# Layer 2's involution pass: queues in the order of the text, norm chains in two steps a turn

## The chip, the cores and the metric

The kernel runs on one core of one Trainium2 chip. The metric is the device time of one execution in microseconds (us). The kernel before took 11256.58 us, the median of three runs (11229.98 to 11261.98). A profile is one further execution under the hardware profiler; its instruction times are shown in us from the start of its span.

Five engines have queues of their own and run each queue in order: TensorE (PE, with its weight loads PEld), VectorE (DVE), ScalarE (ACT), GpSimd (POOL) and SyncE (SP), which in this kernel issues all the DMAs.

## The reference

Sixteen images of 64 x 64 pixels and 256 channels, in float32, go through four layers, each of the form `x = x + layer(group_norm(x))`. Only layer 2 matters here, with the end of layer 1 in front of it and the start of layer 3 behind it:

```python
# end of layer 1: batch norm, relu, residual
x = x + relu((x2 - mean) * rsqrt(var + eps) * gamma + beta)
# layer 2, an involution 3 x 3 with 16 groups, on g = group_norm(x)
r   = relu(bn(g @ Wr + br))                    # 256 -> 64
w   = (r @ Ws + bs).reshape(B, H, W, 16, 1, 9) # 9 weights for each pixel and group
xi  = g @ Wi + bi                              # 256 -> 256
out = sum(w * patches3x3(xi), axis=-1)         # 9 products for each output value
x   = x + out
# layer 3 begins with group_norm(x)
```

`group_norm` has 32 groups of 8 channels over all pixels of an image, so nothing that uses a normalised image can start before the last pixel of that image is known.

## The kernel before

Layer 2 is one loop, a software pipeline. An image is cut into 8 chunks of 512 pixels, and a turn of the loop does four jobs on four different chunks (`jobs`, with the lags 0, 9, 17 and 27 turns of `LAG`):

- `end_of_layer1`, in three parts divided by `yield`: VectorE scales x1 by the spatial factors pf (L899, two instructions); ScalarE applies the relu (L905) and GpSimd adds the residual (L908) to give x2, which is stored; VectorE takes statistics of x2 (L914). With an image's last chunk the chain `norm2` is started.
- `projected`: TensorE multiplies x2 by the scaled Wi (L948, tile px), and ScalarE writes the result with its bias into the padded image `pad` (L952).
- The involution, whose inputs are made one turn earlier by `prepare`: `reduced2` (L969, tile pr; ScalarE's relu L972 to rt), `patches` (TensorE transposes shifted rows of `pad`, L995; ScalarE copies them to xs, L999 to L1005) and `weights` (L979, tile pw, one for each half of the channels). In the turn itself `residual` (L1021 and L1023) puts x2 transposed into PSUM tiles lo, `products` (L1033, 12 VectorE instructions for a half, tile pd) multiplies patches and weights, `sums_on_tensor` (L1050, 18 matmuls) sums the nine taps of one quarter of the first half into lo, and `sums` reduces the rest on VectorE (L1045) and adds lo (L1046). A turn later ScalarE copies the quarter that TensorE summed (L1175), `turned` transposes the result back (L1060, ScalarE copies it to c3, L1061) and hands out its stores, and `statistics3` takes statistics (L1080), which with an image's last chunk starts the chain `norm3`.
- `centred`: GpSimd subtracts the mean for layer 3 (L1103), and 32 DMAs of 22 or 28 KB write the result into `strips`, layer 3's overlapping columns.

The stores of a turn are collected in the list `stores` and issued by SyncE at the start of the next turn (L1150), behind the loads for that next turn (`loads`, L867) and ahead of `load_centred` (tile xc). Most loaded tiles have two buffers; a load waits until all that use the older tile of its slot are done.

`norm2` and `norm3` are generators, as is `group_norm` which they call: group means and deviations through small matmuls with gmat (L117 and L126, tiles pg and pv), an inverse square root with GpSimd's power (L99), then the scaled weights (L924, L925) and their biases (L931, tile pm; L936 and L938), or for `norm3` the saved means and scales (L1087, L1088) and a broadcast of the mean (L1092, L1095 with tile pb, L1098). `step()` moves each running chain to its next `yield`; the loop calls it six times a turn.

None of this text order binds. A scheduler in the compiler orders each engine's queue by dependencies and its own estimates of durations, and takes the order of the text only as a preference. In the trace the queues therefore differ from the text: VectorE's reductions (L1045) stand behind the statistics L914, and pr stands behind `sums_on_tensor`.

[...] the pool `tr` has two (transposes pt, and px), `sm` one (pr and all small tiles of the chains), `pwp` three (pw) and `acc` two (lo).

Of the kernel before, what the change touches and what calls it, by code (L numbers as in the profile page):

```python
# [15 lines left out]
P = 128  # L16
# [28 lines left out]
def network(ctx: ExitStack, tc: tile.TileContext, a: dict, out: bass.AP):  # L45
# [60 lines left out]
            if next(c, c) is c:  # L106
                chains.remove(c)

    def group_norm(stats, pool):


        mv = small.tile([P, 2, 2], F32, tag="gn_mv", name="gn_mv")
        for h in range(2):
            nc.vector.bn_aggr(mv[:, h, :], stats[:, h].rearrange("p n s -> p (n s)"))
        yield
        pg = pool.tile([P, CT], F32, tag="sm", name="pg")
        nc.tensor.matmul(pg[:, 0:2], lhsT=gmat, rhs=mv[:, :, 0], start=True, stop=True)  # L117
        gm = small.tile([P, 2], F32, tag="gn_m", name="gn_m")
        nc.vector.tensor_copy(gm, pg[:, 0:2])
        dev = small.tile([P, 2], F32, tag="gn_d", name="gn_d")  # L120
        nc.vector.tensor_tensor(dev, mv[:, :, 0], gm, ALU.subtract)
        nc.vector.tensor_tensor(dev, dev, dev, ALU.mult)
        nc.vector.tensor_tensor(dev, dev, mv[:, :, 1], ALU.add)
        yield
        pv = pool.tile([P, CT], F32, tag="sm", name="pv")
        nc.tensor.matmul(pv[:, 0:2], lhsT=gmat, rhs=dev, start=True, stop=True)  # L126
        rstd = small.tile([P, 2], F32, tag="gn_r", name="gn_r")
        inv_sqrt(rstd, pv[:, 0:2], GN_EPS)
        yield
        return mv, gm, rstd  # L130

    def normalised(dst, src, gm, rstd, nb):
# [16 lines left out]
    with ExitStack() as st:  # L149
# [80 lines left out]
                chains.append(norm0(i))  # L230

        def norm0(i):
            _, gm, rstd = yield from group_norm(st0.pop(i), sm)
            nb = small.tile([P, 2], F32, tag="gn_b", name="gn_b")
            nc.vector.tensor_tensor(nb, gm, rstd, ALU.mult)
            nc.vector.tensor_scalar(nb, nb, -1.0, None, ALU.mult)
            gn0[i] = (gm, rstd, nb)
# [215 lines left out]

        def gate1(i):

            mv, gm, rstd = yield from group_norm(st1.pop(i), sm)
            av = small.tile([P, 2, 2], F32, tag="av", name="av")
            nc.vector.tensor_copy(av[:, :, 0], mv[:, :, 0])
            nc.vector.tensor_reduce(av[:, :, 1], mxs.pop(i), AX.X, ALU.max)
            for h in range(2):  # L460
                nc.vector.tensor_scalar(
                    av[:, h, :], av[:, h, :], gm[:, h : h + 1], rstd[:, h : h + 1],
                    ALU.subtract, ALU.mult,
                )
            yield
            ph = sm.tile([P, CT], F32, tag="sm", name="ph")
            for h in range(2):
                nc.tensor.matmul(
                    ph[0:16, 0:2], lhsT=w1T[:, h, :], rhs=av[:, h, :], start=(h == 0), stop=(h == 1)
                )  # L470
            hr = small.tile([16, 2], F32, tag="hr", name="hr")
            nc.vector.tensor_scalar(hr, ph[0:16, 0:2], 0.0, None, ALU.max)
            hs = small.tile([16, 1], F32, tag="hs", name="hs")
            nc.vector.tensor_tensor(hs, hr[:, 0:1], hr[:, 1:2], ALU.add)
            yield
            pg = sm.tile([P, CT], F32, tag="sm", name="pgate")
            for h in range(2):
                nc.tensor.matmul(
                    pg[:, h : h + 1], lhsT=w2T[:, h * P : (h + 1) * P], rhs=hs, start=True, stop=True
                )  # L480
            gate = small.tile([P, 2], F32, tag="gate", name="gate")
            nc.scalar.activation(gate, pg[:, 0:2], AF.Sigmoid)
            nc.vector.tensor_tensor(ab[:, 0, i, :], rstd, gate, ALU.mult)
            nc.vector.tensor_tensor(gate, gm, ab[:, 0, i, :], ALU.mult)
            nc.vector.tensor_scalar(ab[:, 1, i, :], gate, -1.0, None, ALU.mult)
            nc.vector.tensor_copy(gm1[:, i, :], gm)
# [335 lines left out]
    with ExitStack() as st:  # L822
# [1 line left out]
        wk = st.enter_context(tc.tile_pool(name="b_work", bufs=2))  # L824
        xs_p = st.enter_context(tc.tile_pool(name="b_xs", bufs=6))
        pd_p = st.enter_context(tc.tile_pool(name="b_pd", bufs=2))
        tr = st.enter_context(tc.tile_pool(name="b_tr", bufs=2, space=PSUM))
        sm = st.enter_context(tc.tile_pool(name="b_sm", bufs=1, space=PSUM))
        pwp = st.enter_context(tc.tile_pool(name="b_pw", bufs=3, space=PSUM))
        acc = st.enter_context(tc.tile_pool(name="b_acc", bufs=2, space=PSUM))  # L830
        gmb = {}
# [60 lines left out]
        def end_of_layer1(i, rc):  # L892
# [21 lines left out]
                nc.vector.bn_stats(st0[i][:, h, rc, :], x2[:, h])  # L914
            if rc == NCH - 1:
                chains.append(norm2(i))

        def norm2(i):

            _, gm, rstd = yield from group_norm(st0.pop(i), sm)  # L920
            wrs = wk.tile([P, 2, 64], F32, tag="wrs", name="wrs")
            w = wk.tile([P, 2, C], F32, tag="wis", name="wis")
            for h in range(2):
                nc.vector.tensor_scalar(wrs[:, h], wr2[:, h], rstd[:, h : h + 1], None, ALU.mult)  # L924
                nc.vector.tensor_scalar(w[:, h], wi[:, h], rstd[:, h : h + 1], None, ALU.mult)  # L925
            yield
            pm = sm.tile([P, CT], F32, tag="sm", name="pm")
            for f in range(3):
                for h in range(2):
                    lhsT = wrs[:, h] if f == 2 else w[:, h, f * P : (f + 1) * P]  # L930
                    nc.tensor.matmul(  # L931
                        pm[0 : 64 if f == 2 else P, f : f + 1], lhsT=lhsT, rhs=gm[:, h : h + 1],
                        start=(h == 0), stop=(h == 1),
                    )
            b2 = small.tile([64, 1], F32, tag="b2", name="b2")
            nc.vector.tensor_scalar(b2, pm[0:64, 2:3], sb2[0:64, 2:3], sb2[0:64, 1:2], ALU.mult, ALU.add)  # L936
            bis = small.tile([P, 2], F32, tag="bis", name="bis")
# [24 lines left out]
        def reduced2(i, rc):  # L962
# [1 line left out]
            wrs, b2, _, _ = gn2[i]  # L964
            rt = rts[rc % 2]
            x2 = taken("x2r")
            pr = sm.tile([P, CT], F32, tag="sm", name="pr")
            for h in range(2):
                nc.tensor.matmul(  # L969
                    pr[0:64, :], lhsT=wrs[:, h, :], rhs=x2[:, h], start=(h == 0), stop=(h == 1)  # L970
# [105 lines left out]
        def statistics3(i, rc, c3):  # L1076
# [3 lines left out]
                nc.vector.bn_stats(st3[i][:, oh, rc, :], c3[:, oh].rearrange("p g t -> p (g t)"))  # L1080
            if rc == NCH - 1:
                chains.append(norm3(i))

        def norm3(i):

            _, gm, rstd = yield from group_norm(st3.pop(i), sm)
            nc.vector.tensor_copy(gm3[:, i, :], gm)  # L1087
            nc.vector.tensor_copy(rs3[:, i, :], rstd)  # L1088
            gmb[i] = wk.tile([P, C], F32, tag="gmb", name="gmb", bufs=1)
# [1 line left out]
            for h in range(2):  # L1091
                nc.vector.tensor_scalar(dg[:, h], ident, gm3[:, i, h : h + 1], None, ALU.mult)  # L1092
            yield
            pb = sm.tile([P, CT], F32, tag="sm", name="pb")
            nc.tensor.matmul(  # L1095
                pb[:, 0:C], lhsT=ones, rhs=dg.rearrange("p h c -> p (h c)"), start=True, stop=True
            )
            nc.vector.tensor_copy(gmb[i], pb[:, 0:C])  # L1098

        def centred(i, rc):  # L1100
# [20 lines left out]

        LAG = (0, 9, 17, 27)
        TURNS = NI * NCH + LAG[3]

        def jobs(n):
# [11 lines left out]
            if end:  # L1139
                load_layer1(*end)  # L1140

        loads(0)
        ahead, made, ending, last_end = None, None, None, None
        for n in range(TURNS):
            end, proj, inv, cen = jobs(n)
            nxt = jobs(n + 1)[2]
            done, stores[:] = list(stores), []
            loads(n + 1)
            for dst, src in done:
                nc.sync.dma_start(out=dst, in_=src)  # L1150
            nxt_cen = jobs(n + 1)[3]
            if nxt_cen:
                load_centred(*nxt_cen)
            now, ahead = ahead, None
            last_end, ending = ending, end_of_layer1(*end) if end else None
            if ending:
                next(ending)
            if last_end:
                next(last_end, None)
            if inv:  # L1160
                w1 = weights(now[1], 1)
                x3 = wk.tile([P, 4, C], F32, tag="x3", name="x3", bufs=3)
            step()

            def prepare():
                x2r, rt = reduced2(*nxt)
                ahead = [x2r, rt]
                ahead.append(patches(*nxt, lambda: ahead.append(weights(rt, 0))))
                return ahead

            if nxt and nxt[1]:
                ahead = prepare()
            step()
            if made:
                nc.scalar.copy(made[2][:, 0:ON_PE, 0:P], made[3][:, 0:ON_PE])  # L1175
            if ending:
                next(ending)
            if inv:
                los = residual(now[0])
            c3 = turned(*made[:3]) if made else None  # L1180
            step()
            if proj:
                projected(*proj)
            if inv:
                pd = products(0, now[2], now[3])
                sums_on_tensor(pd, los[0])
            step()
            if nxt and not nxt[1]:
                ahead = prepare()
            if inv:  # L1190
                pd1 = products(1, w1, now[3])
                sums(0, pd, los[0], x3)
            if made:
                statistics3(*made[:2], c3)
            step()
            if inv:
                sums(1, pd1, los[1], x3)
            made = (*inv, x3, los[0]) if inv else None
            step()
            if cen:  # L1200
                centred(*cen)
        for dst, src in stores:
            nc.sync.dma_start(out=dst, in_=src)

    gates.close()

# [306 lines left out]
```

## Time and profile before

| | |
|---|---|
| median of three runs | 11256.58 us |
| the profiled execution | 11230.29 us |
| its span, first to last instruction | 11228.4 us |
| mean granted clock of TensorE | 0.878 |
| busy over the span: PE, PEld, DVE, ACT, POOL | 76%, 55%, 67%, 42%, 9% |
| layer 2, first L899 to last store of strips | 4169 to 8042 us |
| first products L1033, last sum L1046 | 4286.70 us, 7883.35 us |

A row of a view gives the start, the length, the engine, the line of the kernel, the operation, the tile written and the tile read, their shapes, and how many alike are merged; brackets hold the idle time of the engine just before and what ended it. A row of the waits reads: who waited, for whom, how many us in total, how often, and the longest. The rows that follow busy time by stretch are explained where they are shown. SPq marks a DMA issue on SyncE's queue.

### The profile page before, as it was taken

What the parts mean: (1) busy time and instruction counts of PE and PEld (TensorE: products, weight loads), DVE (VectorE), ACT (ScalarE), POOL (GpSimd) and SP (SyncE); (2) the same over time, 40 slices, a digit from 0 to 9 for tenths busy, and PEclk for the clock granted to TensorE, in tenths of its full rate; (3) what the DMA queues carried; (4) which work ended last, traced back from release to release, by engine and by line L of the source; (5) the groups of instructions that cost most, each with busy time, mean ns of one, the idle gap of its engine ahead of it and who ended that gap; (6) DMA issues with size and microseconds to landing.
All of it is one profiled execution on the core that took longest, in us unless ns stands there. A gap on an engine that the chain in (4) does not pass through costs nothing.

```text
span 11228.4 us, 218020 instructions
## 1 busy us (share of the span) xinstructions
PE 8510.5 (76%) x88184; PEld 6175.2 (55%) x88184; DVE 7531.5 (67%) x11694; ACT 4699.1 (42%) x10571; POOL 1065.1 (9%) x681
## 2 busy tenths in 40 slices
PE   8889888988886407777777777777277777778777
PEld 5666666666664205555555555555165656666555
DVE  5566656656665498988888888899254545555444
ACT  4555555555554004333333333333144444444444
POOL 0110111111110001111111111111000000000000
PEclk9999999999997558888888888888689998998988
DMA  7334334434432385555555555544356555555555
GB/s 239 129 134 148 130 122 146 139 128 133 145 101 84 106 279 177 160 169 165 163 159 167 160 168 164 163 151 141 107 177 202 185 194 179 179 181 176 195 185 171
DMA packets 1353714, 1796.58 MB, mean 160 GB/s; under 512 B 132875, under 2 KB 1031812, under 8 KB 1351556
## 3 DMA queue, kind: packets, MB, share of 16 engines
q1 hardware_dynamic: 1352708, 1782.63, 49.6%
q8 instruction: 697, 11.42, 0.4%
q14 instruction: 309, 2.53, 0.1%
HBM read 1268.05 MB, written 536.87 MB: 161 GB/s over the span
## 4 chain that ended last, share of the span: by engine, by line
PE 32%; DVE 20%; issue 17%; DMA 10%; ACT 9%; SPq 7%; POOL 4%; POOLq 0%; DVEq 0%; ACTq 0%
PE pa L1347 6%; DVE wm L1303 6%; SPq L1150 5%; PE pq L261 5%; PE pk L1288 4%; PE py L417 4%; DMA c_d<-c 3%; DVE x L1045 3%; PE pr L1256 2%; ACT sq L426 2%; ACT wm L1298 2%; DVE pd L1033 2%; PE px L948 2%; PE pt L995 2%; DMA xc<-x_d 1%
## 5 line engine op out<-in xcount | busy, mean ns | idle before, releaser
L261 PE MATMUL pq<-wq,xn 128*128 128x384 f32 x4096 | 1475.9, 500 | 59.8 <-DVE diag L310 20.9
L1033 DVE TENSOR_TENSOR pd<-xs,pw 128x576 f32<-128x576 f32 (+15 forms) x3072 | 1450.5, 544 | 47.7 <-ACT xs L1001 47.7
L1303 DVE TENSOR_TENSOR wm<-pk,spanb 128x704 f32<-128x704 f32 x896 | 1148.4, 1344 | 217.4 <-PE pk L1288 217.1
L1288 PE MATMUL pk<-rt,span 64*128 64x176 f32 x12288 | 1175.6, 329 | 153.5 <-DVE wm L1303 61.0
L1347 PE MATMUL pa<-wm,xw 126*32 126x48 f32 x45056 | 819.6, 227 | 474.2 <-issue 374.1
L1288 PEld LDWEIGHTS pk<-rt,span 64*128 64x128 f32 x12288 | 938.1, 188 | 385.7 <-ACT wm L1298 181.8
L1298 ACT ACTIVATE wm<-pk,spanb 128x176 f32<-128x176 f32 x2560 | 975.0, 542 | 337.8 <-PE pk L1288 328.9
L1045 DVE TENSOR_REDUCE x<-pd 128x384 f32<-128x3456 f32 (+1 forms) x256 | 1109.2, 4334 | 0.0
L1347 PEld LDWEIGHTS pa<-wm,xw 126*32 126x32 f32 x45056 | 679.8, 124 | 714.2 <-issue 516.7
L1357 DVE SCALAR_TENSOR_TENSOR ex<-pa,msk,ex 128x192 f32<-128x192 f32 x704 | 287.2, 416 | 1161.8 <-ACT ex L1356 1159.3
L261 PEld LDWEIGHTS pq<-wq,xn 128*128 128x128 f32 x4096 | 752.8, 194 | 492.5 <-issue 54.1
L995 PE MATMUL pt<-ident,pad 128*128 128x128 f32 x4608 | 759.7, 310 | 244.2 <-ACT pad L952 188.5
L995 PEld LDWEIGHTS pt<-ident,pad 128*128 128x128 f32 x4608 | 593.4, 160 | 422.0 <-ACT pad L952 234.2
L1050 PE MATMUL lo<-pd,ident 128*128 128x128 f32 x2304 | 568.0, 415 | 285.4 <-DVE pd L1033 285.4
L999 ACT COPY xs<-pt 128x512 f32<-128x512 f32 x1152 | 644.8, 586 | 299.1 <-PE pt L995 264.4
L1356 ACT ACTIVATE ex<-pa,msk 128x192 f32<-128x192 f32 x704 | 289.3, 420 | 1019.2 <-PE pa L1347 1016.1
L1050 PEld LDWEIGHTS lo<-pd,ident 128*128 128x128 f32 x2304 | 501.2, 268 | 335.6 <-DVE pd L1033 315.3
L948 PE MATMUL px<-x2p,wis 128*128 128x512 f32 x1024 | 571.7, 708 | 37.5 <-ACT c L1061 23.2
L972 ACT ACTIVATE rt<-pr,b,sb 64x512 f32<-64x512 f32 x128 | 98.9, 772 | 1077.3 <-PE pr L969 1017.5
L417 PE MATMUL py<-wo,oT 128*128 128x256 f32 x2048 | 482.4, 386 | 59.9 <-DVE va L277 45.2
L417 PEld LDWEIGHTS py<-wo,oT 128*128 128x128 f32 x2048 | 378.8, 191 | 135.3 <-PE po L380 49.0
L426 ACT ACTIVATE sq<-y 128x256 f32<-128x256 f32 x512 | 213.2, 416 | 520.2 <-DVE y L422 511.7
(229 smaller groups left out, 13427.4 us busy)
## 6 DMA issues: line engine op xcount, KB each, us to landing
xw<-strips SPq DMA_DIRECT2D x704, 512.0 KB
xn<-x_d SPq DMA_DIRECT2D x256, 512.0 KB
x<-x_d SPq DMA_DIRECT2D x256, 512.0 KB
x_d<-x SPq DMA_DIRECT2D x256, 512.0 KB
strips<-xc SPq DMA_DIRECT2D x3072, 28.0 KB
xin<-in_x SPq DMA_DIRECT2D x256, 256.0 KB
x_d<-xc SPq DMA_DIRECT2D x128, 512.0 KB
xm<-x_d SPq DMA_DIRECT2D x128, 512.0 KB
```

The source lines that it names most:

```text
L261: nc.tensor.matmul(pq[:, dd, 0:384], lhsT=xn[:, h, tok], rhs=wq[:, h, hf * 384 : (hf + 1) * 384], start=(h == 0), stop=(h == 1),)
L417: nc.tensor.matmul(py[:, q, :], lhsT=oT[hf][:, q * P : (q + 1) * P], rhs=wo[:, hf, :], start=(hf == 0), stop=(hf == 1),)
L948: nc.tensor.matmul(px, lhsT=w[:, h, fh * P : (fh + 1) * P], rhs=x2[:, h], start=(h == 0), stop=(h == 1),)
L995: nc.tensor.transpose(pt[:, k, h * P : (h + 1) * P], lines[:, h, rc * 4 + e + k, 2 * j : 2 * j + P], ident,)
L999: nc.scalar.copy(t[:, e : e + 2, 0:C], pt)
L1033: nc.vector.tensor_tensor(pd[:, :, o - oh * P : o - oh * P + n, :], xs[dj][:, di : di + 4, c0 : c0 + 9 * n].rearrange("p r (f k) -> p r f ...
L1045: nc.vector.tensor_reduce(half, pd[:, n:], AX.X, ALU.add)
L1050: nc.tensor.matmul(lo[:, 0:ON_PE], lhsT=ident, rhs=pd[:, 0:ON_PE, :, k], start=False, stop=(k == 8))
L1288: nc.tensor.matmul(pkv[:, b, m], lhsT=span[half, h * 8 + q * 2 + gg, s0 : s0 + P], rhs=rto[half, o, :], start=True, stop=True,)
L1298: nc.scalar.activation(dst[:, m // 2, m % 2], pkv[:, m // 2, m % 2], AF.Identity, bias=spanb[:, g0 + m : g0 + m + 1],)
L1303: nc.vector.tensor_tensor(dst, pkv, spanb[:, g0 : g0 + 4].rearrange("p (b m) -> p b m", b=2).unsqueeze(3).broadcast_to([P, 2, 2, NTL]), AL ...
L1347: nc.tensor.matmul(pav[32 * q : 32 * q + 32, :, tj * TC : (tj + 1) * TC], lhsT=xws[k][0:TILE_IN, tj, 32 * q : 32 * q + 32], rhs=wm[q][0:TI ...
```

## The change

The loop of layer 2 is put under `tc.manual_schedule()`, so that each engine's queue is the order of the text, and the text is rearranged:

- `end_of_layer1` runs its second part after `prepare` and its third (L914) after the last sums of the same turn; before, the third stood in the next turn.
- `step()` is called twice a turn in place of six times: after `turned`, and after the first sums. With `apart=True` the group norm of `norm2` and `norm3` yields between a matmul and the VectorE instructions that read it, so that TensorE's half of a link runs at the first call and VectorE's at the second. Each chain does its first part (L114) at once when it is started.
- `statistics3` moves behind the second `step()`, and `turned` with the copy L1175 stands in front of the first.
- The lags become 0, 12, 20 and 33.
- The pool `sm` is dropped and `tr` gets three banks; pr and the chains' tiles come from `tr`.
- `residual`, `turned`, `projected`, `products` and the two calls of `prepare` (ahead of the residual for chunks 1 to 7 of an image, behind `sums_on_tensor` for chunk 0) keep their order among themselves.

The same instructions are issued for each chunk. The other stages pass a tag to `group_norm` and keep their code.

```diff
-    def group_norm(stats, pool):
+    def group_norm(stats, pool, tag, apart=False):
...
-        pg = pool.tile([P, CT], F32, tag="sm", name="pg")
+        pg = pool.tile([P, CT], F32, tag=tag, name="pg")
         nc.tensor.matmul(pg[:, 0:2], lhsT=gmat, rhs=mv[:, :, 0], start=True, stop=True)
+        if apart:
+            yield
...
-        pv = pool.tile([P, CT], F32, tag="sm", name="pv")
+        pv = pool.tile([P, CT], F32, tag=tag, name="pv")
         nc.tensor.matmul(pv[:, 0:2], lhsT=gmat, rhs=dev, start=True, stop=True)
+        if apart:
+            yield
         rstd = small.tile([P, 2], F32, tag="gn_r", name="gn_r")
         inv_sqrt(rstd, pv[:, 0:2], GN_EPS)
         yield
+        if apart:
+            yield
         return mv, gm, rstd
...
-        tr = st.enter_context(tc.tile_pool(name="b_tr", bufs=2, space=PSUM))
-        sm = st.enter_context(tc.tile_pool(name="b_sm", bufs=1, space=PSUM))
+        tr = st.enter_context(tc.tile_pool(name="b_tr", bufs=3, space=PSUM))
...
                 chains.append(norm2(i))
+                next(chains[-1])
...
-            _, gm, rstd = yield from group_norm(st0.pop(i), sm)
+            _, gm, rstd = yield from group_norm(st0.pop(i), tr, "tr", apart=True)
...
-            pm = sm.tile([P, CT], F32, tag="sm", name="pm")
+            pm = tr.tile([P, CT], F32, tag="tr", name="pm")
...
+            yield
             b2 = small.tile([64, 1], F32, tag="b2", name="b2")
...
-            pr = sm.tile([P, CT], F32, tag="sm", name="pr")
+            pr = tr.tile([P, CT], F32, tag="tr", name="pr")
...
-        LAG = (0, 9, 17, 27)
+        LAG = (0, 12, 20, 33)
...
-            last_end, ending = ending, end_of_layer1(*end) if end else None
-            if ending:
-                next(ending)
-            if last_end:
-                next(last_end, None)
...
-            step()
...
+        with tc.manual_schedule():
+            loads(0)
+            ahead, made = None, None
+            for n in range(TURNS):
+                end, proj, inv, cen = jobs(n)
+                nxt = jobs(n + 1)[2]
+                done, stores[:] = list(stores), []
+                loads(n + 1)
+                for dst, src in done:
+                    nc.sync.dma_start(out=dst, in_=src)
+                nxt_cen = jobs(n + 1)[3]
+                if nxt_cen:
+                    load_centred(*nxt_cen)
+                now, ahead = ahead, None
+                ending = end_of_layer1(*end) if end else None
+                if ending:
+                    next(ending)
+                if inv:
+                    w1 = weights(now[1], 1)
+                    x3 = wk.tile([P, 4, C], F32, tag="x3", name="x3", bufs=3)
...
+                if nxt and nxt[1]:
+                    ahead = prepare()
+                if ending:
+                    next(ending)
+                if made:
+                    nc.scalar.copy(made[2][:, 0:ON_PE, 0:P], made[3][:, 0:ON_PE])
+                if inv:
+                    los = residual(now[0])
+                c3 = turned(*made[:3]) if made else None
+                step()
+                if proj:
+                    projected(*proj)
+                if inv:
+                    pd = products(0, now[2], now[3])
+                    sums_on_tensor(pd, los[0])
+                if nxt and not nxt[1]:
+                    ahead = prepare()
+                if inv:
+                    pd1 = products(1, w1, now[3])
+                    sums(0, pd, los[0], x3)
+                step()
+                if made:
+                    statistics3(*made[:2], c3)
+                if inv:
+                    sums(1, pd1, los[1], x3)
+                if ending:
+                    next(ending, None)
+                made = (*inv, x3, los[0]) if inv else None
+                if cen:
+                    centred(*cen)
+            for dst, src in stores:
+                nc.sync.dma_start(out=dst, in_=src)
```

## The prediction

> **What bounds the kernel now.** I read the 40 slices of the page first: the change touches layer 2 alone, which runs from the first L899 at 4169 us to the last strip store at 8042 us (3873 us of a span of 11228.4). Everything outside keeps its instructions, so I compare this stage with itself. Then the busy time by stretch: four turns before centring begins, two images of eight turns in the middle, and four turns of the last image, where end_of_layer1 has run out.
>
> ```profile
> 4343.00:4440.70 97.70, 80.67 (x410) 59.48 (x409) 97.02 (x136) 43.07 (x86) 10.70 (x9) 0.92 0.46 148
> 5185.40:5420.00 234.60, 170.93 (x815) 121.44 (x814) 202.87 (x298) 82.08 (x162) 39.91 (x26) 0.85 0.53 164
> 5420.00:5656.60 236.60, 171.77 (x815) 123.03 (x814) 206.42 (x298) 81.28 (x162) 39.89 (x26) 0.84 0.53 163
> 7607.30:7695.00 87.70, 70.66 (x360) 49.00 (x358) 87.70 (x122) 29.25 (x62) 9.44 (x4) 0.94 0.56 165
> ```
>
> The columns are the stretch, its length, then PE, PEld, DVE, ACT and POOL busy, the granted clock, the DMA share and GB/s. Early turns take 97.7/4 = 24.4 us with VectorE never idle, late ones 21.9. In the middle an image takes 234.6 to 236.6 us, 29.4 a turn, and VectorE is idle for some 31 us of it (234.6 - 202.9). The waits of VectorE over 4900 to 7400 us (10.6 images) and its queue in one turn say where:
>
> ```profile
> DVE st L914 <- POOL x L908: 235.7, 160, 4.1
> DVE pd L1033 <- ACT xs L1001: 37.7, 22, 2.7
> DVE b L936 <- PE pm L931: 37.4, 11, 3.7
> ```
>
> ```profile
> 5252.60 10.56 DVE L1033 TENSOR_TENSOR pd<-xs,pw 128x468 f32<-128x468 f32 x23
> 5263.08 0.74 DVE L899 SCALAR_TENSOR_TENSOR z<-x,gm,pf 128x512 f32<-128x512 f32 x1
> 5263.86 0.75 DVE L899 SCALAR_TENSOR_TENSOR pf<-x,gm,pf 128x512 f32<-128x512 f32 x1
> 5266.93 0.69 DVE L914 BATCH_NORM_STATS2 st<-x 128x6 f32<-128x512 f32 x1 [2.32 <-POOL x L908]
> 5268.16 0.69 DVE L914 BATCH_NORM_STATS2 st<-x 128x6 f32<-128x512 f32 x1 [0.53 <-POOL x L908]
> 5268.77 3.73 DVE L1045 TENSOR_REDUCE x<-pd 128x384 f32<-128x3456 f32 x1
> ```
>
> The statistics of x2 (L914) stand right behind the L899 pair that they depend on through ScalarE (L905) and GpSimd (L908), and the reduction behind them waits too. That is 235.7/10.6 = 22 us an image; the two other rows add 7. A second resource is nearly as full. The next two fences are SyncE's queue and its waits.
>
> ```profile
> 5246.62 0.35 SPq L867 DMA_DIRECT2D x2p<-x_d  x1
> 5256.61 15.03 SPq L1150 DMA_DIRECT2D strips<-xc  x32
> 5271.75 0.35 SPq L867 DMA_DIRECT2D x2p<-x_d  x1
> ```
>
> ```profile
> SPq L867 <- PE px L948: 334.3, 67, 9.9
> SPq L1150 <- DMA xc<-x_d: 101.4, 163, 1.3
> SPq L1150 <- DMA x_d<-x: 92.7, 212, 1.9
> SPq L1150 <- DMA c_d<-c: 56.5, 144, 1.9
> ```
>
> A turn's 45 DMA issues, 32 of them strips, take 5246.62 to 5271.64, 25.0 us, and only 0.1 us later the next turn starts. Waits of stores for earlier DMAs are part of that: 101.4 + 92.7 + 56.5, some 3 us a turn.
>
> **The change, part by part.** *Order.* In the text, L914 goes behind the second sums, 20 us after L899; GpSimd needs 5 us (5263.08 to 5268.16). So the 22 us an image go. GpSimd's additions then run beside the products: they already do at 4395.87, and 24 products take 11.22 us there, and 0.73 + 10.56 less overlap in the late turns with nothing on GpSimd. I take no cost.
>
> *Norm chains in two steps.* No instruction is added. Per image VectorE has four L114 (1.4 us), eight small copies and sums of 0.16 (1.3), the scalings L924/L925 (1.0), L936/L938 (0.35), L1087/L1088 (0.3 if GpSimd is idle), L1092 and L1098 (1.0): 5.3 us, 0.7 a turn. Their waits (pm 37.4 us above, pg, pv, gn_r) go, since half a turn lies between the halves. The extra turns that the chains take are covered: norm2 ends four turns after L914, and projected now starts five after it (lag 12 against 7); norm3 likewise (28 to 32, centred at 33).
>
> *One PSUM pool of 3 for tr and sm.* A chain's bank is held from TensorE's half to VectorE's, some 12 us, in five or six turns of eight. TensorE then has two banks, as it had before, but pr now shares them; between zero and 2 us in such a turn, mostly inside TensorE's slack; I put 0.1 us a turn.
>
> *TensorE in text order.* The new chain from the turn's start: L899 to 1.5, both L905 to 2.4, the copy L1175 (queued on ScalarE behind L905 now) 2.7, residual 1.2, turned 1.2, projected 3.8, sums_on_tensor 4.4: 13.3 us. L1046 needs that last result after L899, both products and the first reduction: 1.5 + 11.2 + 3.7 = 16.4. Slack 3.1. One turn in eight has none: at rc 7 prepare stands behind sums_on_tensor, and the next turn begins with another prepare. Each is pr 2.0, rt 0.8, nine copies at 0.54 and the small ones, 8.3 us. From 13.3 that gives 21.6, w1 1.0, second prepare 30.9, so 6.5 us into the new turn (24.4) instead of none; L905 cannot start before ScalarE's copies are through. The relus, L1175, residual, turned, projected and sums add 12.4: 18.9 against 16.4, 2.5 us late warm, 5 to 7 with the clock below and the banks. I take 6 us an image, 0.75 a turn.
>
> *The clock.* The row to weigh is projected, eight matmuls, in an early and a middle turn:
>
> ```profile
> 4418.35 3.83 PE L948 MATMUL px<-x2p,wis 128*128 128x512 f32 x8
> 5241.24 5.34 PE L948 MATMUL px<-x2p,wis 128*128 128x512 f32 x8
> ```
>
> [...] By the warm row the chain ends at 13.3 and a turn costs 24.4 + 0.7 + 0.1 + about 0.7 = 25.9; [...] I take 26.5.
>
> *SyncE.* Same 45 issues, new order: loads, stores, strips, then xc. xc reuses the slot of the strips just issued and must wait for the last to land: 1.5 us from issue less 0.4 (worked out from the landings in the trace), so 25.0 + 1.2 = 26.2. The wait for px (334.3 us) goes, for x2p now waits for a projection one turn back. If stores wait less, 24; if the 3 us of waits double, 29. I take 26.2, just covered by 26.5. If VectorE were faster, this would be next.
>
> *Lags.* Three more turns in front of the first product: end-only turns take 5.4 us (4206.32 to 4211.70), some with projection more; the 17 before took 117.5 (4169.2 to 4286.7), I expect 125: +8. Behind the last sum, three more turns of centring, each SyncE's:
>
> ```profile
> 7907.81 1.24 SPq L867 DMA_DIRECT2D xc<-x_d  x2
> 7909.09 13.71 SPq L1150 DMA_DIRECT2D strips<-xc  x32
> ```
>
> Before, 7883.4 to 8042.2 is 158.8 us, 10.4 such turns of 15.2. After, 13.4 turns at 16.4 (the wait for the last strip is bare here): 220, +61. Nothing hides it: TensorE idles 154.98 us there before layer 3.
>
> *Sum.* Now 128 product turns take 4286.7 to 7883.4, 3596.7 us. After: 13 without centring at 26.0 plus 6 to start, 344; 95 full at 26.5, 2518; 20 without end_of_layer1 (21.9 + 0.3 norm + 0.6) at 22.8, 456; together 3318, -279. With +8 and +61: -210. The profiled execution, 11230.3 us with 1.9 around the span, would become 11020. It lies 26 below the median 11256.6, so I predict 11256.6 - 210 = 11047, say **11045 us**.
>
> **Rivals.** *VectorE alone* (0.19): TensorE and SyncE stay hidden, turns are 25.2 full, 22.3 late: 3166, -430 + 61: 10890. For it: the early stretch is 97.02 of 97.7 busy. Against: the double prepare.
>
> *SyncE's queue becomes the turn* (0.17): 45 issues with more waits among the big transfers make 27.8: 95 x 1.3 = 124 more, 11170. For it: 25.0 of 25.1 us used today.
>
> *SyncE's queue, slower than before* (0.07): the wait for strips in front of xc, then x1 and pf behind it, arrives late at L899, and the 3 us of DMA waits triple: 30.5 a turn, 95 x 4 = 380 more, 11425. It decides from 210/95 = 2.2 us more than forecast, 28.7 a turn. Against: L899's loads stand a turn ahead.
>
> *It doesn't do what it says* (0.05): order was not the cause, full turns stay at 29.4, only the lags are paid: 11320.
>
> **How the numbers follow.** My case has 0.52, and 10980 to 11110. A measurement here tells about 0.3% (34 us) from no change. Range 10930 to 11210: it holds my case, SyncE's turn, and part of VectorE alone, and leaves out 0.2. Faster: 0.52 + 0.19 + 0.17 less a tail of 0.03 that ends within the bound: 0.85; same those 0.03; slower 0.07 + 0.05 = 0.12.
>
> **What would show it.** Right: L914 without a wait for POOL; an image near 212 us with VectorE busy 203; one turn in eight near 31 with L1046 waiting for PE lo L1050; SyncE's xc waiting for strips; bare drain near 220. Wrong: an image over 230 us, or L899 waiting for DMA pf. If L1046 waits each turn, the cold chain was undersized; if nothing waits, the double prepare was oversized.

## The result, and the profile after

The changed kernel takes 11136.69 us (median of 4 runs, 11126.9 to 11149.55) against 11253.7 us (4 runs) for the kernel before on the same chip: a ratio of 0.99, 95% interval 0.9882 to 0.9919. It is 117 us faster where 210 had been forecast. The profiled execution took 11132.22 us, with a span of 11130.4 us and a granted clock of 0.88; profile against profile the gain is 98 us, and layer 2's pass holds nearly all of it. Its parts (fill: first L899, now L904, to the first product; products: to the last sum; drain: to the last strip), in us:

| | before | after | forecast | measured |
|---|---|---|---|---|
| fill | 117.5 | 130.1 | +8 | +12.6 |
| 128 product turns | 3596.6 | 3402.5 | -279 | -194.1 |
| drain | 158.8 | 245.0 | +61 | +86.2 |
| pass | 3872.9 | 3777.5 | -210 | -95.4 |

So all three terms have the forecast sign, and all three came out worse than forecast. Lines have moved in the changed kernel: L899 is L904, L908 is L913, L914 is L919, L1033 is L1040, L1045/L1046 are L1052/L1053, L1050 is L1057, L867 is L872, L1150 is L1160. In the runs of the next section they lie one or two off these.

The first view is the busy time of one image (eight turns) in the middle, with the columns explained above.

```profile
6009.50:6229.50 220.00, 161.73 (x774) 116.91 (x772) 199.13 (x287) 76.99 (x154) 40.32 (x26) 0.84 0.57 174
```

The image takes 220.0 us instead of about 235, but VectorE is still idle for 21 of them; the forecast was 212. Its queue in one turn shows that the old wait is gone:

```profile
5044.68 0.69 DVE L1053 TENSOR_TENSOR x<-x,lo 128x512 f32<-128x512 f32 x1
5045.28 1.28 DVE L919 BATCH_NORM_STATS2 st<-x 128x6 f32<-128x512 f32 x2
...
5047.92 11.23 DVE L1040 TENSOR_TENSOR pd<-xs,pw 128x576 f32<-128x576 f32 x24
```

The statistics L919 stand behind the last sum L1053, with no bracket: nothing is waited for, and VectorE's waits have no row of L919 left. The rows that took its place, over 4900 to 7200 us (10.5 images):

```profile
PE pr L976 <- DMA x2r<-x_d: 248.1, 61, 6.9
...
DVE x L1053 <- PE lo L1057: 121.2, 52, 4.8
```

TensorE now waits for a load, x2r, some 24 us an image, and VectorE for TensorE some 11.5 us. Loads come late because SyncE's queue has no gap left. One of its turns:

```profile
5002.80 1.27 SPq L872 DMA_DIRECT2D xc<-x_d  x2
5004.11 0.61 SPq L872 DMA_DIRECT2D x2p<-x_d  x1
...
5012.97 15.49 SPq L1160 DMA_DIRECT2D strips<-xc  x32
5029.66 1.27 SPq L872 DMA_DIRECT2D xc<-x_d  x2
```

From xc to the next xc it is 26.9 us here, and 27.49 over 80 turns (5004 to 7203 us), with some 0.3 us a turn of waiting for a computing engine. In the kernel before, the same queue stood 3.9 of 29.4 us a turn waiting for px. A turn of the drain; the next begins at 7818.36 us, and the later ones take 16.2 to 16.8 us for the 16.4 forecast:

```profile
7801.70 1.24 SPq L872 DMA_DIRECT2D xc<-x_d  x2
7803.27 13.75 SPq L1160 DMA_DIRECT2D strips<-xc  x32
```

### The profile page after: what moved, and what is told of

It reads as the page before. It is cut to its first block, busy times and chain, and to the rows that moved or that the text cites. A ratio compares the mean times of both kernels' runs of the same rounds, so it can differ in the third digit from the quotient of the medians.

```text
span 11130.4 us, 218459 instructions
## 1 busy us (share of the span) xinstructions
PE 8373.7 (75%) x88184; PEld 6128.7 (55%) x88184; DVE 7525.9 (68%) x11694; ACT 4689.9 (42%) x10571; POOL 1069.2 (10%) x681
## 4 chain that ended last, share of the span: by engine, by line
PE 32%; DVE 18%; DMA 15%; issue 13%; SPq 10%; ACT 9%; POOL 3%; DVEq 0%; ACTq 0%; POOLq 0%
SPq L1160 8%; PE pa L1353 6%; DVE wm L1309 6%; PE pq L267 5%; DMA c_d<-c 5%; PE pk L1294 4%; DMA x<-x_d 4%; PE py L423 4%; PE pr L1262 2%; ACT sq L432 2%; SPq L872 2%; ACT wm L1304 2%; PE px L955 2%; DMA strips<-xc 2%; DVE y L428 1%
## 5 line engine op out<-in xcount | busy, mean ns | idle before, releaser
L1040 DVE TENSOR_TENSOR pd<-xs,pw 128x576 f32<-128x576 f32 (+15 forms) x3072 | 1438.0, 549 | 4.5 <-PE pw L986 2.8
L1052 DVE TENSOR_REDUCE x<-pd 128x384 f32<-128x3456 f32 (+1 forms) x256 | 1110.9, 4339 | 0.0
L1006 ACT COPY xs<-pt 128x512 f32<-128x512 f32 x1152 | 606.8, 589 | 117.5 <-PE pt L1002 115.5
L1002 PEld LDWEIGHTS pt<-ident,pad 128*128 128x128 f32 x4608 | 532.4, 149 | 215.3 <-issue 155.6
L1002 PE MATMUL pt<-ident,pad 128*128 128x128 f32 x4608 | 618.2, 289 | 19.1 <-ACT xs L1006 7.7
L976 PE MATMUL pr<-x2r,wrs 128*64 128x512 f32 x512 | 362.9, 849 | 324.0 <-DMA x2r<-x_d 324.0
L1057 PE MATMUL lo<-pd,ident 128*128 128x128 f32 x2304 | 552.7, 409 | 3.7 <-DVE pd L1040 3.7
L955 PE MATMUL px<-x2p,wis 128*128 128x512 f32 x1024 | 520.8, 653 | 20.5 <-ACT pad L959 10.1
L1057 PEld LDWEIGHTS lo<-pd,ident 128*128 128x128 f32 x2304 | 474.9, 207 | 107.7 <-issue 54.8
L1030 PE MATMUL lo<-ident,x2r 128*128 128x128 f32 x896 | 181.7, 330 | 464.0 <-ACT x L1183 294.6
```

The lines of the kernel that those rows point to most:

```text
L955: nc.tensor.matmul(px, lhsT=w[:, h, fh * P : (fh + 1) * P], rhs=x2[:, h], start=(h == 0), stop=(h == 1),)
L1002: nc.tensor.transpose(pt[:, k, h * P : (h + 1) * P], lines[:, h, rc * 4 + e + k, 2 * j : 2 * j + P], ident,)
L1040: nc.vector.tensor_tensor(pd[:, :, o - oh * P : o - oh * P + n, :], xs[dj][:, di : di + 4, c0 : c0 + 9 * n].rearrange("p r (f k) -> p r f ...
L1052: nc.vector.tensor_reduce(half, pd[:, n:], AX.X, ALU.add)
L1057: nc.tensor.matmul(lo[:, 0:ON_PE], lhsT=ident, rhs=pd[:, 0:ON_PE, :, k], start=False, stop=(k == 8))
```

## The experiments

Two theories of the kernel before stood at the start. O: the order of VectorE's queue set its turn, and SyncE's queue sets it only after the change. B: SyncE's queue set it before as well, and the late statistics only filled time that the queue had left. In the recorded expectations "theory S" speaks of the changed kernel: SyncE's queue sets its full turn; its rival T is that TensorE's chain does. Turns are means of all product turns from the 20th to the 107th: 29.46 us in the kernel before, 27.25 in the changed one. Waits and stretches come from the profiled execution of each run.

**xc behind the other loads.** In the changed kernel, a turn's xc is loaded behind the other loads of its own turn and ahead of the stores, in place of behind the strips of the turn before, so that it no longer waits for the strips just issued.

```diff
                 loads(n + 1)
+                if cen:
+                    load_centred(*cen)
                 for dst, src in done:
                     nc.sync.dma_start(out=dst, in_=src)
-                nxt_cen = jobs(n + 1)[3]
-                if nxt_cen:
-                    load_centred(*nxt_cen)
```

> The changed kernel, but SyncE issues the load of xc behind the turn's other loads and not straight behind the last strip store, so that it no longer waits there (1.37 us a turn in the trace of the changed kernel, between the last strip and xc). The same issues, the same work. Theory S (SyncE's queue sets the full turn, 27.5 us now): the full turn falls to about 26.1, 95 turns give 130 us, the bare drain falls from 16.3 to 15.2 a turn, 14 us: about 10995 us. Rival T (TensorE's chain with its cold clock and the double prepare sets the turn, and SyncE waits only because it has time): full turns stay at 27.5, only the drain gains: about 11120 us.

Measured: 11140.83 us, ratio 0.9904 (0.9888 to 0.9921), turn 27.35: no gain, and near the numbers that T expected. The gap behind the strips fell from 1.37 to 0.11 us, but one turn in eight took 36 to 40 us, where gmb, which has one buffer, waits for the last centring of the image before:

```profile
DVE gmb L1107 <- POOL xc L1112: 109.7, 10, 13.3
```

That wait could be the reason or could stand in for another, so it was taken away in a further run:

**xc early, two buffers for gmb.** The same with `name="gmb", bufs=2`.

> The changed kernel with xc issued behind the turn's other loads and ahead of the stores, and two buffers for gmb instead of one. Theory (SyncE's queue sets the full turn; with xc ahead of the strips it no longer waits for them, and the one turn in eight of 36 to 40 us was gmb's copy waiting for the last use of the only gmb): all full turns near 26.2 us, no turn in eight above 33, time near 11000 us, L1107 no longer among VectorE's waits. Rival (the image's turn has a second late arrival, the double preparation or xc's landing, that takes the place of gmb's wait): mean turn stays near 27.5 and the time near 11130.

Measured: 11128.54 us, ratio 0.9876 (0.9858 to 0.9895), turn 27.22. The turns of 36 us and the gmb row went, and the mean stayed: the rival's numbers, though its reason isn't shown, since SyncE's turn still has no gap. Most of what the early xc saved came back inside the stores, whose three x_d issues now take 1.39 us each on average instead of 0.62:

```profile
5061.42 5.04 SPq L1162 DMA_DIRECT2D x_d<-x  x3
```

The queue's length is thus no sum of waits that can be removed one by one. In the last 20 product turns, where end_of_layer1 has run out, the early xc did gain, 24.52 to 23.02 us a turn. But layer 3, which no edit here touches, took 3220.3 us instead of 3184.9, and no run tells why.

**Strips on two queues, changed kernel.** Half of the strips go to ScalarE's queue.

```diff
-                            xc[g * HW + lo : g * HW + hi, :, h * P : (h + 1) * P],
+                            xc[g * HW + lo : g * HW + hi, :, h * P : (h + 1) * P], h,
...
-                for dst, src in done:
-                    nc.sync.dma_start(out=dst, in_=src)
+                for dst, src, *h in done:
+                    (nc.scalar if h and h[0] else nc.sync).dma_start(out=dst, in_=src)
```

> The changed kernel, but the strips of the second half of the channels (16 of the 32 a turn) are issued on ScalarE's DMA queue. Theory S: SyncE's turn falls from 27.5 to about 20.5 (16 x 0.44 less), and what lies under it sets the turn: 25.2 if VectorE alone, 26.5 with the double prepare, so 95 to 220 us from full turns, 20 us from the 20 last products, and 100 us from the drain, where 14 turns of 16.3 halve: 10800 to 10920 us, with one turn in eight near 31 us if the double prepare is real. Rival T: full turns stay at 27.5, the drain alone gains: about 11035 us.

Measured: 11302.81 us, ratio 1.0044 (1.0029 to 1.0059), turn 29.56. It got slower, which neither theory had expected, and the waits say how:

```profile
ACT rt L979 <- DMA strips<-xc: 729.1, 67, 21.1
...
PE pt L1002 <- ACT rt L979: 368.4, 81, 13.9
DVE x L1053 <- PE lo L1057: 354.3, 56, 16.5
```

In text order ScalarE's issues stand at the start of its turn. While they wait for earlier DMAs to land, its copies wait behind them, then TensorE, then VectorE. This run says nothing on SyncE; it needed a second queue that holds up nobody.

**Strips on two queues, kernel before.** The same edit in the kernel before.

> The kernel before, with the same split of the strips over SyncE's and ScalarE's DMA queues. If the scheduler's order of VectorE's queue is what cost the time there (L914 behind L899), full turns stay near 29 us and the drain of 158.8 us loses some 75: about 11180 us. Rival (SyncE's queue made the turn of the kernel before too, and VectorE's wait at L914 was its echo): full turns fall to 25 to 26 us: about 10850 us.

Measured: 10884.71 us, ratio 0.9672 (0.9658 to 0.9687), turn 25.66. In the nine turns or so of 5185 to 5420 us VectorE is idle for 1.6 us in all:

```profile
5185.00:5420.00 235.00, 188.25 (x926) 138.30 (x925) 233.44 (x336) 93.81 (x184) 46.09 (x29) 0.87 0.60 183
```

By itself this spoke for B. But its VectorE queue shows that the order had changed too:

```profile
5268.83 0.67 DVE L1046 TENSOR_TENSOR x<-x,lo 128x512 f32<-128x512 f32 x1
5269.43 0.73 DVE L899 SCALAR_TENSOR_TENSOR pf<-x,gm,pf 128x512 f32<-128x512 f32 x1
5270.09 1.27 DVE L914 BATCH_NORM_STATS2 st<-x 128x6 f32<-128x512 f32 x2
```

L914 stands behind the last sum, with no wait. With issues on ScalarE the scheduler had planned another order (of VectorE's 4759 instructions in the pass, 1240 match those of the kernel before in sequence). So this run changed two things, which the next runs part.

**The scheduler's order.** The changed kernel with the scheduler back, keeping lags, chains and pools.

```diff
-        with tc.manual_schedule():
+        with ExitStack():
```

> The changed kernel without the manual schedule: the rearranged text, the chains in two steps, one PSUM pool and the longer lags stay, but the compiler's scheduler orders the queues again. Theory S with the order as the gain: full turns go back to 28.5 to 29.4 and the lags cost 97 us (fill 11, drain 86 in the changed kernel): 11280 to 11350 us. Rival (the rearranged text is enough, the manual schedule adds nothing): about 11137 us.

Measured: 11356.32 us, ratio 1.0091 (1.0076 to 1.0106), turn 30.30, fill 133.2 and drain 214.2. The turn is even above the 28.5 to 29.4 expected. L919 waits for GpSimd again, and SyncE's x2p for px, so its queue had room (waits over 4900 to 7300 us):

```profile
DVE st L919 <- POOL x L913: 328.4, 89, 6.7
SPq L872 <- PE px L955: 418.5, 69, 12.3
```

The text order is what shortens the turn; lags, chains and pools without it only cost.

**16 strips of twice the bytes, kernel before.** The channel halves lie side by side in `strips`, so that the same bytes leave in 16 issues. Layer 3 reads them in runs of 512 bytes instead of 4 KB.

```diff
-    strips = dram.tile([NI, 2, HW + 9, TC + 6, NTC, P], ...
+    strips = dram.tile([NI, HW + 9, TC + 6, NTC, 2, P], ...
...
-                    for h in range(2):
-                        stores.append((
-                            strips[i, h, r0 : r0 + 4, c0 : c0 + hi - lo, tj, :].rearrange(
-                                "r w c -> w r c"),
-                            xc[g * HW + lo : g * HW + hi, :, h * P : (h + 1) * P]))
+                    stores.append((
+                        strips[i, r0 : r0 + 4, c0 : c0 + hi - lo, tj].rearrange(
+                            "r w h c -> w r (h c)"),
+                        xc[g * HW + lo : g * HW + hi]))
```

> The kernel before with the same 16 issues of twice the bytes. Theory (in the kernel before, too, SyncE's queue was the bound, and the late x2 statistics behind GpSimd's were the scheduler's answer to it): turn near 25.7 as with the strips on two queues, drain near 130, no wait of L914 for GpSimd, time near 10870. Rival (a second queue helped, not fewer issues): turn near 29.4, time near 11250.

Measured: 11255.27 us, ratio 0.9987 (0.998 to 0.9993), turn 29.46, equal to the kernel before to two places. The expectation, which had followed B, failed. SyncE's issues fell from 19.0 to 12.7 us a turn; two of its rows, and the image of eight turns:

```profile
5285.43 8.24 SPq L1149 DMA_DIRECT2D strips<-xc  x16
5303.61 0.35 SPq L867 DMA_DIRECT2D x2p<-x_d  x1
```

```profile
5191.10:5425.70 234.60, 170.91 (x814) 121.46 (x814) 202.88 (x298) 82.15 (x162) 39.97 (x26) 0.85 0.55 164
```

Now 9.9 us stand free between the last strip and x2p (11.0 a turn on average), and the image takes the same 234.6 us with the same 202.9 of VectorE as before the change. VectorE's instructions have the same order as in the kernel before (all 4759 in the pass match in sequence), and the wait is the same:

```profile
DVE st L914 <- POOL x L908: 235.8, 160, 4.1
```

against 235.7 us before, over the same stretch. That is the experiment that decides between O and B: with the order kept and the queue relieved, the turn doesn't move. (The ratio just below 1 is the drain, 62 us shorter, against layer 3, 80 us longer.)

**16 strips of twice the bytes, changed kernel.** The same edit.

> The changed kernel with the two channel halves side by side in strips, so that a turn stores the same bytes with 16 issues in place of 32, each of twice the bytes; the last layer then reads strips in runs of 512 bytes in place of 4 KB. Theory (the number of SyncE's issues sets the turn): SyncE's turn falls from 27.5 by about 16 x 0.49 to near 19.6 us, the turn becomes VectorE's 26.2 (25.2 to 26.5), the drain's last 13 turns fall from 16.3 to about 9, so the drain from 245 to 160 or so; time 10900 to 11000, more if the last layer's reads get longer. Rival (it is the bytes and their landing that hold the queue): turn stays near 27.6, time near 11130. Second rival (the changed order leaves another wait just beneath, PE's for x2r or VectorE's for lo): turn near 27, time near 11060.

Measured: 10951.58 us, ratio 0.9722 (0.9708 to 0.9737), turn 25.88, drain 141.0. One image, and SyncE's queue:

```profile
4985.00:5191.20 206.20, 161.61 (x810) 121.45 (x809) 199.65 (x293) 80.57 (x161) 40.18 (x26) 0.86 0.63 187
```

```profile
5029.94 1.27 SPq L872 DMA_DIRECT2D xc<-x_d  x2
5037.51 0.35 SPq L872 DMA_DIRECT2D x2p<-x_d  x1
```

SyncE is free for 6.3 us behind xc (5.8 a turn on average), so its turn is 20.1 us against 19.6 expected, and VectorE is idle for 6.6 us of an image in place of 21. Half the issues with the same bytes shorten the turn, so it is the issues and not the bytes that hold the queue, and T is refuted with it: TensorE's instructions and their order are the same. The same relief that was worth 6 us of products in the kernel before is worth 155 us here (3402.5 to 3247.9). The time is in the middle of the range expected, although layer 3 pays: from the last strip to the end it takes 3268.7 us against 3184.9.

**Both: 16 strips, xc early, two gmb.**

> The changed kernel with both: 16 issues, and xc ahead of the stores with two gmb. Theory (once SyncE's queue has slack, where xc stands in it is worth nothing): within 0.3% of the changed kernel with 16 issues alone, 10900 to 11000. Rival (xc's late landing holds GpSimd and through it VectorE): 40 us or more below it.

Measured: 10961.07 us, ratio 0.9734 (0.972 to 0.9749), turn 25.87, as expected: with room in the queue, xc's place is worth nothing.

**A quarter of the strips on ScalarE's queue.** As two queues in the changed kernel, with `h and tj > 3` in place of `h`.

> The changed kernel with only 8 of a turn's 32 strips on ScalarE's queue. Theory: SyncE's turn falls by 8 x 0.49 to about 23.6, below VectorE's 25.9, but ScalarE's 8 issues still wait for transfers ahead of its copies; the turn lies between, near 27, time near 11050. Rival (any strip on ScalarE's queue waits for a landing, and that blocks TensorE as 16 did): turn near 29.5, time near 11300. Second rival (8 issues fit into ScalarE's idle time): turn 25.9, time near 10880.

Measured: 11194.51 us, ratio 0.9937 (0.992 to 0.9953), turn 27.97: neither the theory's 27 nor either rival. Eight issues hold up ScalarE less than sixteen (316.8 us of rt waiting for strips, over 4900 to 7100), but still cost more than SyncE gains.

**Half of the strips on GpSimd's queue.** As two queues in the changed kernel, with `nc.gpsimd`.

> The changed kernel with half of the strips (16 of 32 in a turn, those of the second channel half) issued from GpSimd's queue, which has work of some 5 us a turn here, in place of ScalarE's, whose waiting issues held up TensorE. Theory (SyncE's queue alone holds the changed kernel's turn above VectorE's 25.9, and a second queue gives that back when its waits block no engine on the path): turn near 25.9 us, layer 2's pass near 3520 us as with 16 issues, and no longer reads in the last layer, so time near 10870. Rival (GpSimd's own issue of a strip is so much dearer than SyncE's 0.49 us, 1.4 us or more, that its queue is the turn): turn above 28, time 11250 or more.

Measured: 10906.0 us, ratio 0.9685 (0.967 to 0.9699), turn 25.88, pass 3539.0. GpSimd's queue has the room (issues included, GpSimd is busy for 111.9 of the 208 us from 5006):

```profile
5035.66 4.87 POOL L1160 DMA_DIRECT2D strips<-xc  x9 [0.29 <-POOL xc L1112]
```

An issue takes 0.55 us there. The turn is the same 25.88 as with 16 issues, although two different edits relieved SyncE, and layer 3 keeps its reads (3174.7 us). The time is 36 us above the 10870 expected; 19 of them lie in the pass (3539.0 for 3520).

**16 strips on two queues, kernel before.** Eight of the 16 on ScalarE's queue.

> The kernel before with 16 issues of twice the bytes, 8 of them on ScalarE's queue. Theory (the scheduler gives the good order, with the x2 statistics behind the last sum, once ScalarE issues strips; SyncE's length is not what made the difference): turn near 25.7, drain near 95, the last layer's reads longer by about 80 as in the kernel before with 16 issues alone, so time near 10920. Rival (the good order came with 16 issues on ScalarE only by their length, and 8 leave the old order): turn near 29.4, time near 11250.

Measured: 10909.95 us, ratio 0.9688 (0.9671 to 0.9705), turn 25.76, drain 92.1, as expected. Eight issues on ScalarE brought the good order as sixteen had. Why the scheduler plans it then, and not with 16 issues on SyncE alone, no run tells.

Put side by side, the 128 product turns in us:

| | SyncE's queue as it was | relieved (16 issues) |
|---|---|---|
| the scheduler's old order | 3596.6 (before) | 3590.5 |
| order of the text | 3402.5 (after) | 3247.9 |

So 6 us from the second limit alone, 194 from the first alone, 349 from both. The second row also has the changed lags, chains and pools; the run with the scheduler's order shows that these alone gain nothing.

## Why the prediction was right or wrong

The sign and the cause were right: the order held the turn, L914's wait was the largest part of what it cost, and the text order removed that wait. (No run put L914 alone back, so its share of the gain isn't parted from the rest of the order.) Theory B, which I came to hold after the first runs, was refuted by the kernel before with 16 issues. The size was off by 93 us. The result lies outside the interval of my own case, 10980 to 11110; it is inside the stated range because that held the rival of SyncE's turn too, and this rival is what came.

*Order.* Right: no wait of L919, and GpSimd's additions run beside the products at no cost (24 products take 11.23 us, against 11.22 forecast).

*SyncE.* This step failed: "Same 45 issues, new order ... so 25.0 + 1.2 = 26.2 ... just covered by 26.5". The strips' gap was right, 1.37 us for 1.2. The 25.0 was not, for two reasons. It is one turn; the mean over 4900 to 7200 us, less the wait for px, was already 25.5 (29.4 - 3.9). And SyncE had waited for px just ahead of it. Without that pause the loads take longer, 5.4 us a turn with xc instead of 4.6 (each pf issue 0.85 us instead of 0.46, x2p 0.62 instead of 0.35), the strips with their gaps 15.9 instead of 15.5, and the stores 4.8 instead of 5.3. That makes 27.5, close to the 27.8 of the rival "SyncE's queue becomes the turn". It is the issues themselves that take longer. The waits for earlier DMAs did not grow: leaving out xc's, they are 3.5 us a turn before and after (296 us over 4900 to 7400, 297 over 4900 to 7200). With 16 issues, where the queue pauses again in the same order, pf is back at 0.47 and x2p at 0.36. What makes an issue longer in a queue without a pause, no run tells.

The rival's place in my order of chances was too low; its price of 11170 was 33 above the result, my forecast 92 below. The middle turns are 27.25 instead of 26.5 (88 x 0.75 = 66 us), and the last 20 are 24.52 instead of 22.8 (34 us), because SyncE's queue is full there too. One of its turns takes 24.8 us:

```profile
7458.20 1.27 SPq L872 DMA_DIRECT2D xc<-x_d  x2
7483.01 1.27 SPq L872 DMA_DIRECT2D xc<-x_d  x2
```

The first 19, at 25.88, gave 11 back, and the very last, at 22.6, counted as a full one in my sum, 4. That is the 85 us missing in the products.

*VectorE.* With SyncE relieved, its turn is 25.88 where 26.5 had been forecast. Busy time is 199.65/8 = 25.0, as forecast (24.4 + 0.7). L1053 waits for TensorE 42.4 us over 10.4 images, 4.1 us an image for the 6 taken, and only in the turn of the double prepare (3.2 us) and the one ahead of it; the order of its price was right.

*The clock.* Oversized. I had charged 0.5 to 0.6 us a turn for a slower clock on TensorE's chain, part of projected included; the charge was an estimate of mine, shown by no trace. Only the difference between the two rows of projected was shown: a granted clock of 1.00 over the 3.83 us of the early turn, 0.68 over the 5.34 of the middle one. In the changed kernel projected is busy for 3.60 to 3.96 us in each of five turns from 5185 us:

```profile
5185.41 3.70 PE L955 MATMUL px<-x2p,wis 128*128 128x512 f32 x8
```

That is near the 3.83 us of the early turn and not the 5.34 of the middle before; the granted clock over the row is 1.00, at an unchanged mean of 0.84 for the image. The 5.34 was one of two kinds before: over 4900 to 7200 us, 44 of 78 turns took about 3.7 us at a granted clock of 1.00, the other 34 took 4.97 to 6.69 us at 0.64 on average, and the mean was 4.58; in the changed kernel it is 4.07. With 16 issues it is 4.48, so projected is partly slow in many turns, but outside the double prepare and the turn ahead of it VectorE doesn't wait for the chain. So the slow clock is real, and its price on the path was near nothing: the sum by the warm row, 25.9, meets the 25.88 measured, the sum with my charge, 26.5, doesn't. With 25.9 the forecast would have put VectorE's turn under SyncE's 26.2.

*Norm chains.* Their waits are gone, and the chains' cost lies inside the 25.0 us. What the two steps are worth apart from the order wasn't tried.

*Lags.* Fill +12.6 for +8, drain +86 for +61. The bare turn was right. But the turns around the last sum, up to 7753 us, take 20 to 24 us each, since SyncE issues the products' own stores and loads for layer 3 in them; I had counted 13.4 turns all of the bare length. With the queue relieved in both kernels, the lags' price in the drain is 141.0 - 96.7 = 44 us.

Of "what would show it": L919 came free of waits, and SyncE's xc waits for strips. Three sizes failed: an image of 220.0 us for 212, a drain of 245 for 220, and one turn in eight of 28.4 for 31. L904 waiting for pf, a sign of being wrong, shows in a trace: 5.1 us over 10.5 images.

## What to carry to other kernels

Where two resources are nearly full, removing the first limit pays only down to the second, and each cure tried alone misleads: here a relief of SyncE was worth nothing before the order was changed and 155 us after. A queue's length read from one turn behind a pause was too short here by 1.1 us without its gap (25.0 for 26.1); take the mean over many turns and, where there is one, a stretch without pauses, and give the rival that it becomes the turn as much weight as the margin (26.2 against 26.5) deserves. Under a scheduler, an edit that moves DMA issues to another engine can change the whole order, so compare the order before reading the time; the fastest kernels here are the one before with strips on two queues (10884.71 us, or 10909.95 with 16 issues) and the changed one with half of them on GpSimd's queue (10906.0 us), whose intervals of the ratio overlap.

## What the runs showed of the hardware

- Worked out from the records of the changed kernel over 5004 to 7203 us: strips land 2.05 us after issue, x2p, x2r, x1, pf and the stores 5.7 to 6.9. None of the 3600 issues on SyncE's queue in this stretch began before the DMA issued eight before it had landed, and in 659 of them (8.2 a turn) that landing came over 50 ns after the issue just ahead had ended. Waiting for it held the queue for 3.6 us a turn in the kernel before and in the changed one, and 3.8 with xc early and two gmb, so it doesn't account for the longer turn.
- The time of an issue itself was not fixed, as a mean by run: pf takes 0.46 us in the kernel before, 0.85 in the changed one and 0.45 with xc early, x_d 0.57, 0.62 and 1.39.
- The 740 clock records of the kernel before show TensorE's granted clock at 1.0 and 0.5 in turn, and each begins a whole number of 3.413 us behind the first, to within 1 ns. In stretches of that length, one in which TensorE was busy for less than 0.4 was followed by one at 0.5 in all of 444 cases; between 0.4 and 0.6 in 187 of 281, between 0.6 and 0.8 in 116 of 620, above 0.8 in 58 of 1937. So in this trace half clock also followed stretches that were far from idle.
- With 16 of a turn's strips on ScalarE's queue in the changed kernel, its copies stood behind issues that waited: rt waited 729.1 us for strips in 4900 to 7400 us. On GpSimd's queue an issue took 0.55 us against 0.39 on SyncE's, and VectorE's turn is 25.88, as with 16 issues on SyncE's queue alone.
- The same strips read in runs of 512 bytes instead of 4 KB made the last part of the kernel some 84 us longer (3184.9 to 3268.7), while halving the number of strip stores. The size is rough: the nine profiles with runs of 4 KB lie between 3174.7 and 3220.3, the four with 512 bytes between 3241.5 and 3268.7.
